# Loading x in pieces of 112, m and 16 - m rows, in a kernel that multiplies pairs of features

## The chip, the cores and the metric

The kernel runs on one core of a Trainium2 chip. The metric is the time of one execution on the device, in microseconds (us). The kernel before took 1336.87 us (median of two runs, 1336.65 and 1337.08). The profile is of one more execution, whose span from the first to the last instruction is 1335.1 us.

## The reference

There are 4096 samples, each with 32 feature vectors of 64 numbers (float32). For each of the 496 pairs (i, j) with i < j, the vector i is multiplied by a 64 x 64 matrix that belongs to the pair, and the product is multiplied element by element with the vector j:

```python
# inputs (4096, 32, 64), W (496, 64, 64)
i_idx, j_idx = np.triu_indices(32, k=1)
vi = inputs[:, i_idx, :]
vj = inputs[:, j_idx, :]
vdotw = jnp.einsum('bpd,pde->bpe', vi, W)
inter = vdotw * vj
return inter.reshape(B, -1)          # (4096, 31744)
```

The output is 520 MB; the inputs are 33.6 MB (x) and 8.1 MB (W).

## The kernel before

The samples go through in 32 tiles of 128. A sample is a row on one of the 128 partitions of SBUF, the memory on the chip. W stays in SBUF. For each tile TensorE transposes x (eight 128 x 128 blocks to a group, two groups), ScalarE (ACT) copies the transposes from PSUM to SBUF, TensorE multiplies them with the matrices, and VectorE (DVE) multiplies what lands in PSUM with x and writes into `ring`, a buffer of 28,160 columns. From there four stores per tile go to the output, of 7552, 6528, 7872 and 9792 columns.

x has three slots of one tile each in SBUF. After the first tile it comes two tiles at a time, so that one row on a partition is 2 x 2048 numbers, 16 KB:

```python
F32 = mybir.dt.float32
P = 128
STORES = [[0, 1], [2, 3], [4, 5, 6], [7, 8, 9, 10, 11, 12, 13, 14, 15]]
FIRST_HALF_AT, SECOND_HALF_AT = 9, 3
RING = 28160

def x_slots(NT):
    # for NT = 32: [(0, slot 0)], then [(1, 1), (2, 2)], [(4, 0), (3, 1)], [(5, 1), (6, 2)], ...
    # 17 loads: the first and the last have one tile, the 15 between them two
    loads = [[(0, 0)]]
    for t in range(1, NT, 2):
        ...
    return loads

# [...]
    xbuf = const.tile([P, 3 * F * D], F32, tag="x", name="x")
    x_loads = x_slots(NT)

    def load_x(load):
        at = sum(len(before) for before in x_loads[: x_loads.index(load)]) * P * F * D
        n = len(load) * F * D
        s = load[0][1]
        nc.scalar.dma_start(
            out=xbuf[:, s * F * D : s * F * D + n],
            in_=x[at : at + P * n].rearrange("(p c) -> p c", p=P),
        )
```

The loads are issued from ACT's queue, the stores and the loads of W from SyncE's (SP). A load is issued at the beginning of the tile ahead of the first tile that it brings; that tile is first transposed at pair 9 of the tile ahead:

```python
    transpose_x(slot[0], 0)
    for t in range(NT):
        xt = slot[t]
        for load in x_loads:
            if min(load)[0] == t + 1:
                load_x(load)
        for s, group in enumerate(STORES):
            if at + store_w[s] > RING:
                at = 0
            osb = ring[:, at : at + store_w[s]]
            at += store_w[s]
            for p in group:
                if p == SECOND_HALF_AT:
                    transpose_x(xt, 1)
                if p == FIRST_HALF_AT and t + 1 < NT:
                    transpose_x(slot[t + 1], 0)
                # [...] matmuls into PSUM; products with x into osb
            nc.sync.dma_start(
                out=out[:, t * cols + o0 : t * cols + o0 + store_w[s]], in_=osb
            )
```

Each transfer of this kernel has 128 rows, one for each partition.

Of the kernel before, what the change touches and what calls it, by code (L numbers as in the profile page):

```python
# [1 line left out]

# [6 lines left out]

F32 = mybir.dt.float32  # L10
ALU = mybir.AluOpType

P = 128
BANK = 512
BANKS = 8

STORES = [[0, 1], [2, 3], [4, 5, 6], [7, 8, 9, 10, 11, 12, 13, 14, 15]]

LOADS = [[0], [1], [2, 3], [4, 5, 6], [7, 8, 9, 10, 11, 12, 13, 14, 15]]
# [11 lines that stand above are left out]
        if t + 1 == NT:  # L31
            loads.append([(t, 1)])
        elif loads[-1][-1] == (t - 1, 2):
            loads.append([(t + 1, 0), (t, 1)])
        else:
            loads.append([(t, 1), (t + 1, 2)])
    return loads


@with_exitstack  # L40
def pair_bilinear_kernel(
    ctx: ExitStack,
    tc: tile.TileContext,
    x: bass.AP,
    w: bass.AP,
    out: bass.AP,
    F: int,
    D: int,
):

    nc = tc.nc
    NT = out.shape[1] * 2 // (F * (F - 1) * D)
    NPR = F // 2

    width = [(F - 1 - i) * D for i in range(F)]
    off = [sum(width[:i]) for i in range(F)]
    cols = sum(width)  # L80


    woff = [i % 2 * D + sum(width[i % 2 : i : 2]) for i in range(F)]
    store_w = [sum(width[2 * p] + width[2 * p + 1] for p in g) for g in STORES]

    const = ctx.enter_context(tc.tile_pool(name="const", bufs=1))
    psum = ctx.enter_context(tc.tile_pool(name="ps", bufs=1, space=bass.MemoryType.PSUM))

    ident = const.tile([P, P], F32, tag="ident", name="ident")
    make_identity(nc, ident)  # L90

    def runs(tl, a, b, n):

        ap = tl[:, a : a + n]
        return bass.AP(ap.tensor, ap.offset, [list(ap.ap[0]), [b - a, 2], list(ap.ap[1])])

    xbuf = const.tile([P, 3 * F * D], F32, tag="x", name="x")
    x_loads = x_slots(NT)
    slot = {t: xbuf[:, ts(s, F * D)] for load in x_loads for t, s in load}

    def load_x(load):

        at = sum(len(before) for before in x_loads[: x_loads.index(load)]) * P * F * D
        n = len(load) * F * D
        s = load[0][1]
        nc.scalar.dma_start(
            out=xbuf[:, s * F * D : s * F * D + n],
            in_=x[at : at + P * n].rearrange("(p c) -> p c", p=P),
        )

    pring = psum.tile([P, BANKS * BANK], F32, tag="pring", name="pring")
    bank = 0

    def take_banks(n):

        nonlocal bank
        if bank + n > BANKS:
            bank = 0
        got = pring[:, bank * BANK : (bank + n) * BANK]
        bank = (bank + n) % BANKS  # L120
        return got

    xT = const.tile([P, NPR * P], F32, tag="xT", name="xT")

    def transpose_x(xt, g):

        n = 2 * BANK // P
        pt = take_banks(2)
        for c in range(n):
            nc.tensor.transpose(pt[:, ts(c, P)], xt[:, ts(n * g + c, P)], ident)  # L130
        nc.scalar.copy(xT[:, ts(g, 2 * BANK)], pt)  # L131

    ring = const.tile([P, RING], F32, tag="ring", name="ring")
    at = 0

    load_x(x_loads[0])
    w_sb = const.tile([P, sum(width[0::2])], F32, tag="w", name="w")
    done = 0
    for g in LOADS:

        upto = woff[2 * g[-1]] + width[2 * g[-1]]
        nc.sync.dma_start(out=w_sb[:, done:upto], in_=w[:, done:upto])
        done = upto
# [12 lines that stand above are left out]
            o0 = off[2 * group[0]]  # L156
# [5 lines that stand above are left out]
                first = (width[2 * p] - 1) % BANK + 1  # L162
                for c1 in range(first, width[2 * p] + 1, BANK):
                    n = first if c1 == first else BANK
                    c0 = c1 - n
                    odd = width[2 * p + 1] and c1 > D
                    pm = take_banks(2)
                    for h in range(1 + bool(odd)):
                        a = woff[2 * p + h] + c0 - h * D
                        nc.tensor.matmul(  # L170
                            pm[:, h * BANK : h * BANK + n],
                            xT[h * D : (h + 1) * D, ts(p, P)],
                            w_sb[h * D : (h + 1) * D, a : a + n],
                            start=True,
                            stop=True,
                        )
                    xj = xt[:, (2 * p + 1) * D + c0 : (2 * p + 1) * D + c1]
                    o = [off[2 * p + h] - o0 + c0 - h * D for h in range(2)]
                    if odd and (c0 or c1 < width[2 * p]):
                        nc.vector.tensor_tensor(  # L180
                            runs(osb, o[0], o[1], n),
                            runs(pm, 0, BANK, n),
                            bass.AP(xj.tensor, xj.offset, [xj.ap[0], [0, 2], xj.ap[1]]),
                            ALU.mult,
                        )
                    else:
                        for h in range(1 + bool(odd)):
                            nc.vector.tensor_tensor(  # L188
                                osb[:, o[h] + h * D : o[h] + n],
                                pm[:, h * (BANK + D) : h * BANK + n],  # L190
                                xj[:, h * D :],
                                ALU.mult,
                            )
            nc.sync.dma_start(
                out=out[:, t * cols + o0 : t * cols + o0 + store_w[s]], in_=osb
            )


# [30 lines left out]
```

## Time and profile before

| what | value |
|---|---|
| time, median of two runs | 1336.87 us |
| span in the profile | 1335.1 us |
| read from HBM, written to it | 41.94 MB, 520.09 MB |
| rate over the span | 421 GB/s |
| loads of x with two tiles | 15, of 2048 KB each |
| stores | 4 x 32, of 3264 to 4896 KB each |

The profile gives for each engine how long it was busy; PE is TensorE. The span is also cut into 40 slices, with the busy share of each in tenths (9 is 90% or more) and what the 16 DMA engines moved in GB/s. A wait is put down to what ended it: "DVE ring L180 <- DMA out_dram<-ring" is VectorE about to write to the ring on line 180 and kept from it by a store that still reads it. The chain follows the work that ended last back to the start. L106 is the load of x, L130 the transposes, L131 ACT's copies, L170 the matmuls, L180 and L188 the products on VectorE, L194 the stores.

### The profile page before, as it was taken

Reading aid. Unit: us, or ns where it says so; the run is one execution under the profiler, and the core shown is the slowest. Engines: PE = TensorE matmul, PEld = TensorE weight load, DVE = VectorE, ACT = ScalarE, POOL = GpSimd, SP = SyncE. Lnnn points to the kernel's source line nnn. Section 1 sums busy time; section 2 is a strip of 40 time slices with the busy share of each in tenths; the row PEclk is TensorE's granted clock in tenths of the full one; section 3 lists DMA queues with packets and bytes.
Section 4 is the critical chain, followed back from the end, with each engine's and each line's share of the span. In section 5 each row is a group of like instructions: output and inputs, shape, how many; then the busy total and the mean of one; then the engine's idle time right before and its main releaser. Section 6 shows DMA issues by size and latency. Waiting matters only on the chain.

```text
span 1335.1 us, 13080 instructions
## 1 busy us (share of the span) xinstructions
PE 1160.6 (87%) x5376; PEld 544.9 (41%) x5376; DVE 1183.4 (89%) x1376; ACT 66.1 (5%) x65; POOL 0.7 (0%) x6
## 2 busy tenths in 40 slices
PE   6998989989899898998989889798998979989893
PEld 3443334443344443444444444344443434354441
DVE  5998989989899898998989899898998989989894
ACT  0000000000000000000000000000000000000000
POOL 0000000000000000000000000000000000000000
PEclk9999999989899999998989999899999999989997
DMA  9999999999999999999999999999999999999998
GB/s 397 433 430 430 431 428 430 418 433 430 413 425 410 436 414 427 426 414 433 405 432 431 419 429 411 432 426 421 428 413 430 426 407 417 429 421 423 429 425 352
DMA packets 21659, 562.87 MB, mean 422 GB/s; under 512 B 2400, under 2 KB 2400, under 8 KB 2656
## 3 DMA queue, kind: packets, MB, share of 16 engines
q1 hardware_dynamic: 19152, 528.49, 92.8%
q10 hardware_dynamic: 2448, 33.56, 5.9%
q8 instruction: 42, 0.69, 0.2%
q14 instruction: 17, 0.14, 0.0%
HBM read 41.94 MB, written 520.09 MB: 421 GB/s over the span
## 4 chain that ended last, share of the span: by engine, by line
DMA 47%; DVE 38%; issue 9%; PE 5%; DVEq 0%; ACT 0%
DMA out_dram<-ring 46%; DVE ring L180 32%; DVE ring L188 5%; PE pring L170 5%; DMA x<-in_x_dram 1%; DVEq L180 0%; PE pring L130 0%; ACT xT L131 0%; DVEq L225 0%; DVEq L188 0%
## 5 line engine op out<-in xcount | busy, mean ns | idle before, releaser
L170 PE MATMUL pring<-w,xT 64*128 64x512 f32 (+4 forms) x4864 | 1098.4, 564 | 146.4 <-DVE ring L180 133.5
L180 DVE TENSOR_TENSOR ring<-pring,x 128x1024 f32<-128x1024 f32 (+3 forms) x1056 | 1104.1, 1108 | 131.4 <-DMA out_dram<-ring 102.6
L170 PEld LDWEIGHTS pring<-w,xT 64*128 64x128 f32 x4864 | 489.3, 191 | 711.7 <-DVE ring L180 533.0
L131 ACT COPY xT<-pring 128x1024 f32<-128x1024 f32 x64 | 64.8, 1012 | 1224.1 <-PE pring L130 1224.1
L188 DVE TENSOR_TENSOR ring<-pring,x 128x64 f32<-128x64 f32 (+3 forms) x320 | 97.7, 356 | 2.6 <-DMA out_dram<-ring 1.9
L130 PEld LDWEIGHTS pring<-ident,x 128*128 128x128 f32 x512 | 55.6, 142 | 58.8 <-DVE ring L180 50.2
L130 PE MATMUL pring<-ident,x 128*128 128x128 f32 x512 | 70.8, 282 | 8.6 <-DMA x<-in_x_dram 8.6
L131 ACT ACT_TABLE_LOAD x1 | 1.3, 1283 | 1.7 <-PEq L221 1.7
masks.py:199 POOL TENSOR_SCALAR_AFFINE_SELECT ident<-ident 128x128 f32<-128x128 f32 x1 | 0.3, 292 | 0.1
masks.py:197 POOL MEMSET ident<- 128x128 f32 x1 | 0.2, 204 | 0.3 <-POOLq L221 0.3
L221 POOL MEMSET const-bfloat16-1.0<- 128x1 bf16 x1 | 0.1, 101 | 0.0
L221 POOL MEMSET const-uint8-127<- 128x1 uint8 x1 | 0.1, 101 | 0.0
L221 POOL MEMSET const-float32-0.0<- 128x1 f32 x1 | 0.1, 98 | 0.2 <-issue 0.2
L221 POOL MEMSET const-float32-1.0<- 128x1 f32 x1 | 0.1, 98 | 0.0
## 6 DMA issues: line engine op xcount, KB each, us to landing
out_dram<-ring SPq DMA_DIRECT2D x32, 4896.0 KB, 17.7
out_dram<-ring SPq DMA_DIRECT2D x32, 3936.0 KB, 18.1
out_dram<-ring SPq DMA_DIRECT2D x32, 3776.0 KB, 18.3
out_dram<-ring SPq DMA_DIRECT2D x32, 3264.0 KB, 18.6
x<-in_x_dram ACTq DMA_DIRECT2D x15, 2048.0 KB, 20.4
w<-in_w_dram SPq DMA_DIRECT2D x1, 2592.0 KB, 28.1
x<-in_x_dram ACTq DMA_DIRECT2D x2, 1024.0 KB, 12.8
w<-in_w_dram SPq DMA_DIRECT2D x1, 2016.0 KB, 22.2
```

Source lines behind the costliest of these rows:

```text
L130: nc.tensor.transpose(pt[:, ts(c, P)], xt[:, ts(n * g + c, P)], ident)
L131: nc.scalar.copy(xT[:, ts(g, 2 * BANK)], pt)
L170: nc.tensor.matmul(pm[:, h * BANK : h * BANK + n], xT[h * D : (h + 1) * D, ts(p, P)], w_sb[h * D : (h + 1) * D, a : a + n], start=True, st ...
L180: nc.vector.tensor_tensor(runs(osb, o[0], o[1], n), runs(pm, 0, BANK, n), bass.AP(xj.tensor, xj.offset, [xj.ap[0], [0, 2], xj.ap[1]]), ALU ...
L188: nc.vector.tensor_tensor(osb[:, o[h] + h * D : o[h] + n], pm[:, h * (BANK + D) : h * BANK + n], xj[:, h * D :], ALU.mult,)
L221: nc = bacc.Bacc("TRN2", target_bir_lowering=False, num_devices=1)
```

## The change

Seven of the loads with two tiles, number 1 to 7 of the list, come in three transfers in place of one: the first 112 rows, then m rows, then 16 - m rows, where m is the number of the load. The other loads stay as they were, and so does all else. The rows of a transfer are shared out over DMA engines, and the change alters how many rows of x each engine gets.

```diff
@@ def load_x(load):
         n = len(load) * F * D
         s = load[0][1]
-        nc.scalar.dma_start(
-            out=xbuf[:, s * F * D : s * F * D + n],
-            in_=x[at : at + P * n].rearrange("(p c) -> p c", p=P),
-        )
+        rows = x[at : at + P * n].rearrange("(p c) -> p c", p=P)
+        slots = xbuf[:, s * F * D : s * F * D + n]
+        m = x_loads.index(load)
+        pieces = [P - 16, m, 16 - m] if 0 < m < 8 else [P]
+        p0 = 0
+        for k in pieces:
+            nc.scalar.dma_start(out=slots[p0 : p0 + k, :], in_=rows[p0 : p0 + k, :])
+            p0 += k
```

In the order of ACT's instructions the three issues of a load stand in the place of the one, between the same copies; only in load 1 the two small pieces come after ACT's first copy.

## The prediction

> **What bounds the kernel now.** I read four views in this order: the busy table and the slices, the waits, the chain that ended last, and the DMA view of the last 45 us.
>
> From the page of the kernel before, the busy times, the DMA row of the slices and the queues (queue, packets, MB, share of 16 engines):
>
> ```profile
> PE 1160.6 (87%) x5376; PEld 544.9 (41%) x5376; DVE 1183.4 (89%) x1376; ACT 66.1 (5%) x65; POOL 0.7 (0%) x6
> ...
> DMA  9999999999999999999999999999999999999998
> ...
> q1 hardware_dynamic: 19152, 528.49, 92.8%
> q10 hardware_dynamic: 2448, 33.56, 5.9%
> q8 instruction: 42, 0.69, 0.2%
> ```
>
> The 16 DMA engines are busy for 92.8 + 5.9 + 0.2 = 98.9% of the span, VectorE for 89%. The stores (q1) are nearly all of it; the loads of x (q10), which the change touches, are 5.9%. Next the waits (who waited <- for whom: us in total, times, longest us) and the chain's shares:
>
> ```profile
> DVE ring L180 <- DMA out_dram<-ring: 102.6, 44, 6.2
> DVE ring L180 <- PE pring L170: 17.9, 9, 13.5
> ...
> PE pring L130 <- DMA x<-in_x_dram: 8.6, 1, 8.6
> ```
>
> ```profile
> DMA 47%; DVE 38%; issue 9%; PE 5%; DVEq 0%; ACT 0%
> DMA out_dram<-ring 46%; DVE ring L180 32%; DVE ring L188 5%; PE pring L170 5%; DMA x<-in_x_dram 1%; DVEq L180 0%; PE pring L130 0%; ACT xT L131 0%; DVEq L225 0%; DVEq L188 0%
> ```
>
> VectorE waits 44 times for a store to leave the ring, and for x nobody waits after the first load (one wait, 8.6 us, at the start). So the stores' rate sets the time, and loads of x matter only by the DMA time that they take. The loads have room as well. The issues by line say how long a load takes:
>
> ```profile
> x<-in_x_dram ACTq DMA_DIRECT2D x15, 2048.0 KB, 20.4
> ```
>
> A store counts as landed when the last of its engines is done, so the slowest engine decides. That there is a slow one is seen in the last 45 us (40 slices of 1.1 us, busy tenths and GB/s):
>
> ```profile
> DMA  9999999998999898989999992999299992900000
> GB/s 487 419 438 438 430 430 403 430 430 382 398 514 537 371 418 348 471 387 443 443 448 448 448 448 112 543 550 515 104 522 522 557 487 104 557 35 35 35 0 0
> ```
>
> After the last full slice (557 GB/s) three slices move 35 GB/s each: one engine, alone, with its last rows. The trace's record of single DMA packets says more. A packet begins when the one before it on its engine ends, so packets can be chained. Fifteen chains move a row of 31,488 B in 1166 ns and one of 26,112 B in 968 ns; one chain needs about 1200 and 996 ns, and likewise 1133 against 1119 ns (30,208 B) and 1480 against 1448 ns (39,168 B). With 8 rows of each store per engine that chain loses about 8 x (34 + 28 + 14 + 32) ns = 0.9 us in a tile, 1.8 us in the two tiles that one load serves. From 230 us on its part of a store ends 3.6 to 4.9 us after the first engine's. There the lag stops growing: the ring is full, and twice in two tiles the other engines run dry for 0.2 to 1.5 us. The slow engine never does. The span is its work plus the start.
>
> **What the Trainium skill says.** (1) "DMA: Bandwidth & Descriptors", section "Why a DMA increments its semaphore by 16 and not by 1": a transfer issued from the ACT queue uses the largest number of engines up to 16 that divides its slowest dimension that isn't 1, and takes the lowest-numbered ones. The trace before has only transfers of 128 rows and shows 8 rows on each engine. (2) Same page, "Latency and other measured facts": engines 7 and 15 are usually the slower ones, which the page puts down to software descriptor generation. Here all transfers are hardware ones ("hardware_dynamic"), yet one engine is slower by some 2 to 3%; the trace doesn't give its number. (3) "SBUF — State Buffer", section "Door 1: The DMA port swizzle": four neighbouring partitions share a port, and a transfer to partitions 0 to 15 reached 104 GB/s, against 328 for 128 partitions. No transfer of the kernel before shows it: its rows of 16 KB take 611 ns on every quick engine, 26.8 GB/s. (4) "DMA: Bandwidth & Descriptors", section "The descriptor swizzle": in a transfer over 128 partitions each engine has a port of its own, which fits that even 611 ns.
>
> **The change, part by part.** It moves no byte more or less; seven loads of 128 rows of 16 KB become 112 + m + (16 - m) rows.
>
> *Rows per engine.* By (1), 112 rows are 7 on each of 16 engines. The m rows go to engines 0 to m - 1 and the 16 - m rows to engines 0 to 15 - m. Summed over m = 1 to 7 and against 8 rows per load, engine 15 has 7 rows fewer, engine 14 six fewer, and so on to engine 9 with one fewer; 7 and 8 are as before; engine 6 has one more, up to engine 0 with seven more. (By the letter of the rule the single row at m = 1 is cut over all 16 engines, a sixteenth of a row each; I neglect it.)
>
> *If engine 15 is the slow one,* it sheds 7 x 0.62 us (611 ns and its 2%) = 4.3 us. It sheds them one row per load, 0.6 of the 1.8 us that it loses in the same two tiles, so it stays the slowest and its work still sets the span. Engine 0 gains 4.3 us while the slow one loses 7 x 1.8 = 12.6 us, so extra rows alone don't make it the bound. Sum: -4.3 us.
>
> *What the 16 last rows cost.* Partitions 112 to 127 lie on four ports by (3). At 104 GB/s the 262,144 B need an estimated 2.5 us instead of 0.61 us, on every engine that carries one: 1.9 us more per load, and for engines with two rows up to 2 us more again where both rows meet full ports (m = 4 to 7). Summed over seven loads with four rows on a port whenever they could meet, I get some 18 to 20 us more on engines 0 and 1. Against them stands what the slow engine loses in that time anyway, 12.6 us, plus the 4 us by which others may fall behind before anyone waits: 16.6 us. So in the worst case engines 0 and 1 hold up everything for about 4 us beyond the time before; if the rows meet only half of the time (10 us), it is hidden altogether and the 4.3 us stay won.
>
> *112 rows.* Seven rows per engine no longer match groups of four partitions, so two engines can meet on a port there too. If a quarter of the rows took double time, each engine would lose 7 x 0.25 x 0.61 = 1.1 us per load, the slow one too, up to 7 us over all.
>
> *Issues and waits.* Fourteen more issues on ACT at some 366 ns each are 5 us of an engine that is 5% busy. The eight DMA semaphores are taken in turn, so a piece also waits for the transfer eight issues earlier: a store of two tiles (some 80 us) ago, which needed 18 us. Nothing is added to the path. VectorE, TensorE and the stores keep their order.
>
> **The rivals.** *A, relief:* the slow engine is number 15 and sheds 4.3 us: 1332.5. For it: one engine only lags, it never idles, and the ramp of m spares 15 each time. *B, ports:* the rows on four ports eat the relief: 1336 to 1341. For it: the measured figure of (3), and that by the packet records most of the other engines start their x rows within 0.15 us of each other, so that they do meet. Against it: they have slack to lose, and each engine puts a store's packet between two rows of x. *C, the wrong engine or a slower 112-row transfer:* if the slow engine is 7 it sheds nothing and pays for the ports; 1341 to 1347. For it: page (2) names 7 as well. *D, a new wait for x:* a load lands 20.4 us after its issue, and x is first needed at the next tile's transposes, about 29 us later (70% of a tile of 41 us); 3 us more would still fit. I give it little.
>
> **Range and chances.** A 45%, B 35%, C 20%. Weighted with 1332.5, 1338.5 and 1344 that is 1336.9; the middle of the distribution is lower, at the border of A and B. I take 1335.5 us, range 1331 to 1344. Neither way can reach 2% (27 us): the loads concerned are 7/16 of 5.9% of the DMA time, 34 us per engine, and would have to double with nothing hidden. Faster by over 2%: 0.01; within: 0.97; slower by over 2%: 0.02.
>
> **What would show it.** For A: the tail of three slices at 35 GB/s is still there, stores end with the same lag of some 4 us after 230 us, fewer or later dry stretches before 560 us, and packets of 16,384 B at 611 ns. For B: many such packets at 1.2 to 2.5 us in the first 560 us and more waiting of VectorE for stores there. For C: slow packets among the 112 rows too, and more loss per load. I am wrong altogether if the time leaves the range, if VectorE waits for TensorE's transposes of x, or if the pieces use other engines than the rule says.

## The result, and the profile after

The changed kernel took 1349.57 us (median of two runs, 1348.97 to 1350.17) against 1336.87 us. The ratio is 1.0095, with a 95% interval from 1.0076 to 1.0115: 12.7 us slower. The prediction said 1335.5 us, between 1331 and 1344.

The page of the changed kernel, with the lines that answer to those shown of before (the lines of the kernel have moved down by four: VectorE's products are L184 and L192, the matmuls L174):

```profile
PE 1159.0 (86%) x5376; PEld 546.5 (41%) x5376; DVE 1183.7 (88%) x1376; ACT 66.1 (5%) x65; POOL 0.7 (0%) x6
...
q1 hardware_dynamic: 19152, 528.49, 92.4%
q10 hardware_dynamic: 2560, 33.56, 6.2%
...
DMA 47%; DVE 36%; issue 9%; PE 6%; DVEq 0%; SPq 0%
DMA out_dram<-ring 45%; DVE ring L184 31%; PE pring L174 6%; DVE ring L192 5%; DMA w<-in_w_dram 2%; DVEq L184 0%; PE pring L134 0%; SPq L146 0%; DVEq L229 0%; DVEq L192 0%
```

No compute engine has more to do, and the bytes are the same. The DMA engines are still busy for 98.8% of the span, but the span is longer: the packets themselves take longer. New on the chain is the load of W. The waits of the changed kernel (us in total, times, longest) say the same:

```profile
DVE ring L184 <- DMA out_dram<-ring: 109.3, 44, 6.8
DVE ring L184 <- PE pring L174: 22.0, 15, 14.1
...
PE pring L174 <- DMA w<-in_w_dram: 4.6, 2, 3.3
```

VectorE waits as often as before for stores, only 7 us longer, and TensorE now waits for W. The views by time tell where the 12.7 us are lost. First the start: the DMA row (busy tenths) and GB/s of 8 to 52 us in 40 slices of 1.1 us, before:

```profile
DMA  9999999999999998989999999899998999999999
GB/s 391 408 461 471 391 434 448 399 424 426 469 440 455 444 434 377 490 358 452 371 439 439 427 439 439 384 412 421 455 427 380 451 451 404 471 396 458 401 458 458
```

and in the changed kernel:

```profile
DMA  9979998899599999999979899999999999898999
GB/s 325 257 193 286 325 310 220 231 278 131 85 366 363 387 435 449 455 425 469 425 339 528 377 452 573 427 439 412 439 412 439 439 395 407 380 404 380 522 475 505
```

For eleven slices the DMA engines are nearly as busy as before and move 85 to 325 GB/s in place of some 430. That is the time in which load 1 and the loads of W run side by side. By the packet records a row of 7424 B of W took 436 ns on average instead of 281, and a row of x of load 1 999 ns instead of 611. In sum each engine spent 3.1 us more on its rows of load 1 and 2.1 us more on its rows of W. The first store began 5.3 us later than before (35.0 against 29.7 us), and the next stores began as late until load 2.

Then the middle, from the same store of the third tile to the same store of the 14th in both kernels. The columns are the stretch, its length, busy time and count of PE, PEld, DVE, ACT and POOL, the granted clock, the DMA share and GB/s. Before:

```profile
130.00:576.00 446.00, 395.50 (x1842) 184.30 (x1840) 404.40 (x471) 22.27 (x22) 0.00 (x0) 0.97 1.00 425
```

After:

```profile
135.00:588.00 453.00, 398.76 (x1848) 190.58 (x1848) 406.63 (x474) 22.29 (x22) 0.00 (x0) 0.95 0.99 419
```

Seven us are lost here, in the stretch of loads 3 to 7. From the 14th tile's first store to the last tile's both kernels take the same, 735.4 and 735.2 us. The tail shows the late engine as before (1302 to 1346 us):

```profile
DMA  6899999999889999999999994991999499910000
GB/s 285 385 448 448 439 439 439 439 439 387 384 380 526 522 395 380 439 448 453 453 458 429 429 458 172 556 527 64 570 534 570 178 427 534 570 71 36 0 36 0
```

It works alone at 36 GB/s at the end: the change hasn't relieved it.

### The profile page after: what moved, and what is told of

It reads as the page before. It is cut to its first block, busy times and chain, and to the rows that moved or that the text cites. A ratio compares the mean times of both kernels' runs of the same rounds, so it can differ in the third digit from the quotient of the medians.

```text
span 1346.9 us, 13115 instructions
## 1 busy us (share of the span) xinstructions
PE 1159.0 (86%) x5376; PEld 546.5 (41%) x5376; DVE 1183.7 (88%) x1376; ACT 66.1 (5%) x65; POOL 0.7 (0%) x6
## 4 chain that ended last, share of the span: by engine, by line
DMA 47%; DVE 36%; issue 9%; PE 6%; DVEq 0%; SPq 0%
DMA out_dram<-ring 45%; DVE ring L184 31%; PE pring L174 6%; DVE ring L192 5%; DMA w<-in_w_dram 2%; DVEq L184 0%; PE pring L134 0%; SPq L146 0%; DVEq L229 0%; DVEq L192 0%
## 5 line engine op out<-in xcount | busy, mean ns | idle before, releaser
L174 PE MATMUL pring<-w,xT 64*128 64x512 f32 (+4 forms) x4864 | 1096.9, 564 | 159.0 <-DVE ring L184 141.1
L184 DVE TENSOR_TENSOR ring<-pring,x 128x1024 f32<-128x1024 f32 (+3 forms) x1056 | 1104.9, 1110 | 142.4 <-DMA out_dram<-ring 109.3
L174 PEld LDWEIGHTS pring<-w,xT 64*128 64x128 f32 x4864 | 491.0, 191 | 722.1 <-DVE ring L184 534.5
L192 DVE TENSOR_TENSOR ring<-pring,x 128x64 f32<-128x64 f32 (+3 forms) x320 | 97.9, 357 | 2.9 <-DMA out_dram<-ring 2.3
```

The costliest lines, as they stand in the source:

```text
L174: nc.tensor.matmul(pm[:, h * BANK : h * BANK + n], xT[h * D : (h + 1) * D, ts(p, P)], w_sb[h * D : (h + 1) * D, a : a + n], start=True, st ...
L184: nc.vector.tensor_tensor(runs(osb, o[0], o[1], n), runs(pm, 0, BANK, n), bass.AP(xj.tensor, xj.offset, [xj.ap[0], [0, 2], xj.ap[1]]), ALU ...
L192: nc.vector.tensor_tensor(osb[:, o[h] + h * D : o[h] + n], pm[:, h * (BANK + D) : h * BANK + n], xj[:, h * D :], ALU.mult,)
```

## The experiments

Losses and gains are against the kernel before, run beside each experiment (1336.94 us, in the third set 1336.98). The experiments that cut load 2 and later leave load 1 whole unless they say otherwise.

**Where the loss is made: load 1 or the others.**

```diff
# e1: all but load 1                         # e2: load 1 alone
-  if 0 < m < 8 else [P]                     -  if 0 < m < 8 else [P]
+  if 1 < m < 8 else [P]                     +  if m == 1 else [P]
```

> Load 1 in one transfer, loads 2 to 7 in three pieces as in the changed kernel. In the changed kernel the stores run 5.1 us late already at the third tile's first store and 11.8 us late after load 7. Theory ports (a piece's rows land on SBUF ports that belong to other engines, and at the start collide with the load of W as well): the 5 us of the start go, 1343 to 1345 us. Theory ramp (more rows on engines 0 to 6): one row in 28 of the ramp goes, 1347 to 1349. Theory issues (each extra transfer costs, wherever it is): 6/7 of the loss stays, 1347 to 1348.

> Only load 1 in three pieces (112, 1, 15). Theory ports with W: 1341 to 1343 us, nearly all of the loss within the first 55 us. Theory ramp: one row more on engine 0, 1337 to 1338. Theory issues: 1338 to 1339.

Measured: 1343.63 us (ratio 1.0052, 1.0038 to 1.0066) and 1342.12 us (1.0038, 1.0026 to 1.0051). One load of seven makes 5.2 us, the six others 6.7 us; together 11.9 of the 12.7 us. So the cost isn't the same for each extra transfer. The start of the second run looks like that of the changed kernel (8 to 52 us):

```profile
DMA  9899998999669999899998989998999999999899
GB/s 250 216 281 291 272 303 223 283 290 112 109 206 390 424 435 447 381 440 455 473 415 377 490 377 568 446 412 384 412 439 412 439 421 459 475 427 404 380 404 494
```

**Ramp, ports or issues.** One run without the ramp (16 rows, so again 8 rows on each engine), and one with three transfers of all 128 rows:

```diff
# e3: no ramp                                # e4: three pieces by columns, m = 1 to 7
-  [P - 16, m, 16 - m]                       -  rows p0 : p0 + k of 112, m, 16 - m
+  [P - 16, 16]                              +  columns c0 : c0 + k of 2048, 1024, 1024
```

> Loads 1 to 7 as 112 + 16 rows: each engine has 7 + 1 rows as before the change, so no ramp, but the pieces don't fit the ports. Theory ports: as slow as the changed kernel or slower, since 16 rows meet on four ports at once, 1347 to 1352 us. Theory ramp: as before, 1336 to 1338. Theory issues (half as many extra transfers): 1342 to 1344.

> Loads 1 to 7 in three transfers of all 128 rows, of 2048, 1024 and 1024 columns: as many extra transfers and semaphores as the changed kernel, no ramp and no piece off its port. Theory ports: 1336 to 1338.5 us. Theory ramp: the same. Theory issues: 1347 to 1351.

Measured: 1347.95 us (1.0082, 1.0068 to 1.0096) and 1337.73 us (1.0006, 0.9998 to 1.0014). Without a ramp nearly all of the loss is there, 11.0 us; with as many transfers but all partitions in each, it is 0.8 us, and the interval includes none. Nor did the cut by columns slow the rows: one piece of 8 KB and two of 4 KB took 627 ns together (medians 309 and 159), against 611 for a whole row. The start by columns is as fast as before (8 to 52 us):

```profile
DMA  9999999998989899897999999999999998999999
GB/s 440 448 417 456 426 396 468 438 366 364 471 382 500 368 482 452 377 528 302 494 412 412 427 412 412 412 439 408 502 546 404 404 404 380 408 425 458 458 458 458
```

Ramp and issues fall as main causes. What is left is that an engine's rows lie in other partitions than those of a 128-row transfer.

**Is it ports? A row of x with nothing else beside it.** Load 1 was moved behind W on SyncE's queue, so that hardly a store and little of W runs beside it, and then cut in four ways:

```diff
+            eng = nc.sync if m == 1 else nc.scalar
-            nc.scalar.dma_start(...)
+            eng.dma_start(...)
# pieces of load 1: e7 [128], e8 [112, 1, 15], e11 [64, 64], e12 [16] * 8
```

> Control for the next: load 1 whole, but issued on SyncE's queue behind the loads of W. x of tile 1 comes some 15 us later, so its transposes may wait: 1337 to 1345 us, by any theory.

> As the run before, with load 1 split into 112, 1 and 15 rows. Theory that the start is lost because x rows and W's rows meet on ports: hardly any W left beside it, so at most 2 us more than that run. Theory that a split load 1 costs its 5 us wherever it is: 5 us more than that run.

> How long is a row of x of 16 KB where x has the ports to itself? Load 1 behind W in two transfers of 64 rows. Theory ports (two engines per port): most rows about 1.2 us, against 0.61 us for the 128-row load in the control. Theory without ports: 0.61 us. The time of the whole kernel is of no interest here.

> The same with eight transfers of 16 rows (four engines per port). Theory ports: about 2.4 us a row and some 19 us for the load, as 104 GB/s for 16 partitions would have it. Theory without ports: 0.61 us a row.

Measured: 1336.90 us (1.0000, 0.9992 to 1.0009), 1339.34 us (1.0018, 1.0011 to 1.0025), and for e11 and e12 1341.29 and 1346.27 us, one run each. The median row of 16 KB took 615 ns in one transfer of 128 rows, 1010 ns in 112 + 1 + 15, 1268 ns in 64 + 64 and 1876 ns in eight times 16. So the same bytes on the same 16 engines are the slower the fewer partitions a transfer spans. The control (e7, 23 to 43 us, slices of 0.5 us; x runs from 24.3 to 30.7 us, W until 25.1 us, and stores from 29.8 us on):

```profile
DMA  4977999978989694949896995949898999997979
GB/s 207 664 304 328 426 524 459 426 328 360 524 229 295 274 665 181 665 181 577 362 604 302 423 544 242 604 181 604 362 544 362 426 426 418 418 522 313 522 313 522
```

and with eight times 16 rows (e12, the same window; x runs from 24.4 to 40.6 us, W until 25.7 us, and stores from 38.7 us on):

```profile
DMA  7999597779499929994499499479929995989979
GB/s 332 498 338 361 66 229 98 98 98 262 66 131 131 229 33 131 164 229 66 66 229 164 66 131 262 66 98 164 229 33 131 274 335 181 363 363 483 423 302 423
```

While x is alone there, the slices move 33 to 262 GB/s with the DMA engines mostly busy; in the control they move 229 to 524. That fits the port limit of the Trainium skill's page "SBUF — State Buffer", section "Door 1: The DMA port swizzle", from which the expectations took two and four engines per port; in size it is milder than the four that I had expected (1876 in place of 2400 ns). That the rows meet at the ports is still inferred: a cut also changes which rows of x are read from HBM at the same time, and no run changed the one without the other. The cut load 1 behind W costs 2.4 us more than its control, the one beside W 5.2 us: I had said at most 2. So something like half of the loss at the start is there without W beside it, which fits the 3.1 us of x and 2.1 us of W above.

**What a port shared by two engines costs while stores run.**

```diff
# e5: loads 2 to 7
+  pieces = [P // 2, P // 2] if 1 < m < 8 else [P]
```

> Loads 2 to 7 in two transfers of 64 rows. By the skill's port table partitions 0 to 63 reach eight of the 16 ports, so each port has two engines on it. Theory ports: nearly each x row takes up to twice its 611 ns; between them stores go on, so I expect a loss of 10 to 25 us, 1347 to 1362 us, with x packets of about 1.2 us. Rival, odd sizes (what costs is that 112 = 16 x 7 rows breaks some block of the transfer, while 64 = 16 x 4 rows is even): 1337 to 1339 us.

Measured: 1343.59 us (1.0050, 1.0037 to 1.0062), a loss of 6.7 us, less than my 10 to 25. It isn't odd sizes alone, for 64 = 16 x 4 is even. But between stores the rows of x are slowed less than alone: their mean was 720 ns, against 1206 ns alone. They may meet less often there; this wasn't shown.

**Which engine is the slow one.** First, engine 15 was spared for certain, with little cost in ports:

```diff
# e6: loads 2 to 15
+  columns 0 : 2560 in 128 rows; columns 2560 : 4096 in 120 rows and in 8 rows
```

> Is engine 15 the slow one? Loads 2 to 15: the first 2560 columns in one transfer of 128 rows, the last 1536 as 120 + 8 rows, which by the rule go to engines 0 to 14 and 0 to 7. Engine 15 sheds 8 rows of 6 KB per load, 1.8 us, which is what the slow engine loses in two tiles; the others get 0.2 us more and pay the ports for 3/8 of a load, some 0.4 us. If engine 15 is the slow one: up to 14 x 1.2 us won, 1320 to 1331 us, and the single late engine is gone. If another engine is: 14 x 0.6 lost, 1342 to 1348 us, and one engine still 4 us late. If the slow engine can't be relieved because it is the slow port and not the engine: 1337 to 1343.

Measured: 1341.94 us (1.0037, 1.0025 to 1.0050), 5.0 us lost. Engine 15 as the slow one is out, but the time alone doesn't say more: it lies just under what I expected of another engine (1342 to 1348) and within what I expected of a slow port. The tail (1295 to 1339 us) has one late engine as ever:

```profile
DMA  2999999998998998999999992991999499910000
GB/s 107 412 448 448 439 439 439 439 439 384 431 593 384 395 404 380 443 448 453 453 458 458 429 458 115 556 563 64 534 534 570 214 392 534 570 71 36 0 36 0
```

The packets tell more. This is the late chain of this run from 465 to 482 us, with S a store's row, x a row of 6 KB, s. and X. the end marks of a store and of a piece, and the times in ns:

```
S1208 S1199 S1189 x234 s. x234 S1493 x234 S1462 x249 S1502 x242 S1473
x234 S1489 x249 S1504 x242 S1491 X. S1471 x234 s.
```

Its stores' rows are slow (1199 against 1166, 1489 against 1448 ns), and it has nine rows of 6 KB, eight ahead of the X. and one after. By the rule of the prediction nine rows go to engines 0 to 7 alone; engine 15 would have none. In the changed kernel, and in e1 as well, the late chain had nine rows of x in loads 5, 6 and 7 and eight in loads 2, 3 and 4. By the rule only engine 4 has these numbers. Two runs differ in engine 4's row alone:

```diff
# e9: loads 2 to 15                          # e10: loads 2 to 15
+  [P - 16, 4, 12] if 1 < m < 16             +  [P - 16, 5, 11] if 1 < m < 16
```

> Which engine is the slow one? Followed through the packets, the late chain has 9 rows per load in the run before that gave engines 0 to 7 nine rows, and in the changed kernel a second small row from m = 5 on, but not at m = 4: that would be engine 4. This run cuts loads 2 to 15 into 112, 4 and 12 rows: second rows for engines 0 to 3. If engine 4 is the slow one it keeps 8 rows and pays only for ports, about 1 us per load: 1343 to 1352 us, and the late chain shows 8 rows per load.

> The same with 112, 5 and 11 rows: second rows for engines 0 to 4. If engine 4 is the slow one: 14 rows of 0.62 us more on it, 6 to 9 us slower than the run with 112, 4 and 12, and 9 rows per load in the late chain. If it is any other engine: within 1.5 us of that run.

Measured: 1345.37 us (1.0060, 1.0047 to 1.0074) and 1356.40 us (1.0145, 1.0131 to 1.0159). The move of one row per load from engine 11 to engine 4 costs 11.0 us in 14 loads, 0.79 us each: a row (0.62 us) and a little more, and more than the 6 to 9 us that I expected. The late chain has eight rows of x per load in most loads of the first run and nine in those of the second. It isn't that 5 and 11 rows fit the ports worse than 4 and 12: over all engines the rows of x took 1242.8 against 1231.4 us, 0.7 us per engine. VectorE's wait for stores with 112, 4 and 12 rows:

```profile
DVE ring L184 <- DMA out_dram<-ring: 111.5, 42, 6.7
```

and with 112, 5 and 11:

```profile
DVE ring L184 <- DMA out_dram<-ring: 123.5, 44, 7.7
```

The 11 us come back as 12 us of that wait. The slow engine is number 4, and what is put on it is paid in full or a little more.

## Why the prediction was wrong

*What bounds the kernel* held. Stores set the time, one engine sets the stores, and the time is that engine's work. The last pair of experiments shows it better than anything in the profile of before.

*The step that failed first* is "if engine 15 is the slow one, it sheds 4.3 us". The slow engine is number 4. By my own table of rows it gets one row more at m = 5, 6 and 7 and none less: 3 x 0.62 = +1.9 us where I had put -4.3. The runs give 1.7 us (12.7 of the changed kernel less 11.0 without the ramp) or 0.9 us (6.7 in loads 2 to 7 with the ramp, less 11.0 - 5.2 = 5.8 without). From -4.3 to +1.7 this step alone was off by 6.0 us. I had taken the number from the Trainium skill ("DMA: Bandwidth & Descriptors", section "Latency and other measured facts", engines 7 and 15), while the trace gave none. I did hold another engine possible, as rival C, with 7 in mind, and gave it 20%.

*The term that was missing* is the start. My sum treats all seven loads alike, beside stores. Load 1 runs beside W, which is also written into SBUF: 5.2 us. In the packet records of before, W and load 1 share the time up to 15 us, and I didn't ask what a cut load would meet there.

*The term for 112 rows* was there as a quarter of the rows at double time, 1.1 us per load, "the slow one too, up to 7 us over all". Loads 2 to 7 without the ramp cost 5.8 us, 1.0 us each (with the piece of 16 rows). The size is right, but it stood under a rival and not in the sum.

*The 16 last rows* I had at 1.9 us and more per load on every engine that carries one. This was too much while stores run. In loads 2 to 7 of the changed kernel the rows of x took only 81.9, 79.1, 83.6, 84.1, 85.7 and 81.8 us in all, summed over 16 engines, against some 78.3 us for a whole load. What I hadn't foreseen is where the rest is paid: some 31% of the stores' rows that follow a row of x on their engine took over 50 ns longer, against 3 to 4% before. Between the same stores as in the middle stretch above, the 109 us of engine time lost (6.8 us on 16 engines) are 22 us of rows of x, 45 us of longer rows of stores, some 10 us of ten more rows of stores that fall into the stretch, and 32 us of idle engines.

*The sum as the runs have it:* start 5.2 + ports in loads 2 to 7 5.8 + ramp on engine 4 1.7 = 12.7 us. It closes because the last two terms are differences: they assume that 112 + 16 rows cost as much at the start as 112 + 1 + 15 (the first store began 5.3 and 5.5 us late in these two runs). Rival C, at 1341 to 1347, had the direction; without the start it would have held.

*Slips of the working* moved little. The late chain's row of 30,208 B took 1142 ns in the median and not 1133, which leaves 0.9 us per tile; and 18 to 20 less 16.6 us is 1.4 to 3.4 us, not about 4. And the single row at m = 1 wasn't cut over 16 engines: the trace has the transfer as dst_num_elem=[1,1] with an element of 16,384 B, so that there was nothing to divide.

*Right:* that issues and semaphores add next to nothing (0.8 us, within noise), no wait for x, and the rows per engine, by which the slow one could be found.

Left open: why engine 4 needs 2 to 3% longer for its rows, and whether it is the engine or the partitions that it serves in every store (the 42 instruction fetches of queue q8, 41 us in all, are not the reason: they hardly appear in the late chain); how the rows of a 112-row transfer lie on the ports; and whether the longer stores' rows after a row of x are that row's writes still under way, which would fit but wasn't tested. No version was found that beats the kernel before; the whole load 1 behind W equals it.

## What to carry to other kernels

Before a load is shifted between DMA engines, find out which engine is the late one: give two versions that differ in one engine's rows, or count the late chain's rows. A transfer that doesn't span all 128 partitions can cost its neighbours as much as itself; here it cost most where W was loaded beside it. Where one engine sets the time, extra work on it is paid in full, and the rest of the profile hardly moves.

## What the runs showed of the hardware

- One DMA engine, by the rows per engine number 4 of the core's 16, took 1199 to 1204 ns in the median for a row of 31,488 B where the others took 1166; it was so before, in the changed kernel and in e1, e5, e6, e9 and e10. In the kernel before, its last eleven rows took 1166 and 1448 ns, like those of the others.
- A 16 KB row into SBUF took 615 ns in a transfer of 128 rows, 1268 ns in 64 and 1876 ns in 16, with little else running; among stores the 64-row case averaged 720 ns.
- The first row of a store after an engine had run dry (39,168 B) took 2061 to 2075 ns in place of 1448.
- A transfer of a single row of 16 KB (m = 1) was one packet of 16,384 B with one completion record, not cut over 16 engines.
